# Nine sampling rounds for 128 pixels instead of rounds of 14 pixels, in a deformable-convolution network

## The chip, the cores and the metric

The kernel runs on one core of a Trainium2 chip. The metric is the device time of one execution in microseconds; the kernel before takes 7738.43 us, the median of three runs (7737.99 to 7746.72). Times inside the kernel come from one profiled execution.

## The reference

Four layers work on four images of 256 channels and 64x64 pixels, in float32. The change lies in the first layer, a deformable convolution. Each pixel has four groups of 64 channels, and in each group nine sampling points. Every point has an offset and a softmax weight, both computed from the image; it is a bilinear sample, a weighted sum of the four pixels around a place that is not on the grid.

```python
offset = jnp.einsum('nhwc,oc->nhwo', t, off_w) + off_b
mask = jax.nn.softmax(mlog.reshape(n, H, W, G, P), -1).reshape(n, H, W, G * P)
...
img = xpad.transpose(0, 3, 1, 2).reshape(n * G, GC, Hp, Wp)
samp = _grid_sample(img, sg)
...
dout = (samp * mr).sum(-1).reshape(n, G * GC, H * W).transpose(0, 2, 1).reshape(n, H, W, C)
dout = jnp.einsum('nhwc,oc->nhwo', dout, outproj_w) + outproj_b
x2 = _bn(inp + dout, bn2_g, bn2_b, bn2_m, bn2_v, 3)
```

After it come a squeeze-and-excite with a two-layer feed-forward, a linear-attention layer with 5x5 depthwise convolutions, a binarised 3x3 convolution and a non-local attention layer, each with a group norm before it.

## The kernel before

An earlier stage computes, for each image, a table `tab` in DRAM with 256 values for every place and group (the four pixels of a bilinear sample), and a list `s_d` with one row per pixel and point: four row numbers of the table, one for each group, and 16 weights (four groups, four corners). Rows of `s_d` are ordered by pixel, nine in a row for each.

`sample` then goes through an image in rounds. A round takes RP = 14 pixels, that is RS = 126 rows of `s_d`, one on each of 126 partitions. `gathered` (L596) issues four indirect DMAs on POOL (L600), one for each group, each of which fetches 128 rows of 256 values into a buffer `g`; there are seven such buffers. Partitions 126 and 127 fetch rows of the next round, and their weights in the mask are zero. PE then multiplies `g` by weights `wm` (L607): `wm` has one column for each of OB = 16 pixel slots, and in it the weight of a row stands in the column of its pixel (the mask `own`), so that the matmul sums the nine points and one pair of corners. One round is eight such matmuls, into one half of the accumulator `acc`; two rounds (UR = 2) share a half.

`weigh` (L585) makes `wm` for WR = 4 rounds at once on DVE (L591, 128x1024), in one of two buffers, four rounds ahead. After each pair of rounds three steps follow, one slot apart: `moved` (ACT copies the half of `acc` to SBUF, L612), `turned` (PE transposes it into a half of `dp`, L617) and `spread` (ACT copies it into `dT`, two copies of 64 partitions, L632). When a block of BR = 16 rounds (BP = 224 pixels; the last block of an image has 64 pixels in five rounds) is complete, `project` multiplies `dT` by the output projection (PE, L640), `add` adds the residual (DVE, L644) and `finish` applies the batch norm (ACT, L649) and stores the block as `x2` (SP, L652). `dT` has one buffer, so the first `spread` of the next block waits until `project` has read it, and is put one slot later (`j == 2 and r < UR`). An image has 18 blocks of 16 rounds and one of five, 293 rounds; four images have 1172.

`load` (L572) brings the rows of a block from `s_d` into `sl` with two SP transfers (L580 for partitions 0 to 125, L581 for 126 and 127); it is called one block ahead, and `sl` has two buffers. Because L581 reads two rows past the end, `s_d` has 2 x 126 rows more, filled with zeros in `setup` (L249).

The order of instructions on PE, DVE, ACT and POOL is the order in which the program writes them (`manual_schedule` in `run`). A slot is one round: first the steps that fall due in it (`later`), then the gathers and matmuls of the round, then `load` and `weigh`, and then a share of other layers' work. That share comes from `beside` (L1194): work of the other layers is cut into pieces with a cost each and spread evenly over the rounds. Beside image 0 run the first convolution of images 1 to 3 and the offsets of all images; beside image 1 the binarisation of a weight and, from image 0, the feed-forward (first fifth) and the linear attention (the rest); beside images 2 and 3 also the third and fourth layers of images 0 and 1. The total of that work does not depend on the number of rounds. After the last round the rest of images 2 and 3 runs without sampling.

Of the kernel before, what the change touches and what calls it, by code (L numbers as in the profile page):

```python
# [9 lines left out]
F32 = mybir.dt.float32  # L10
# [15 lines left out]
CT = 8  # L26
# [3 lines left out]
RP, WR, UR, BR = 14, 4, 2, 16  # L30
RS, BP = RP * PT, RP * BR
BLOCKS = [(p0, min(BP, HW - p0)) for p0 in range(0, HW, BP)]
OB = 16
# [38 lines left out]
class Net:  # L72
# [127 lines left out]
    def setup(self):  # L200
# [46 lines left out]
        self.s_d = [dt([HW * PT + 2 * RS, G * 5], F32, name=f"sd{n}") for n in im]  # L247
        for n in im:
            nc.sync.dma_start(self.s_d[n][HW * PT:].rearrange("(p r) f -> p (r f)", r=2), self.zero[0:RS, 0:G * 10])  # L249
# [251 lines left out]
    def coordinates(self, bp, n, c, off, ml):  # L501
# [43 lines left out]
        for xt, wx in ((0, w0[:, 0]), (1, loc[:, 0])):  # L545
# [5 lines left out]
            self.s_d[n][0:HW * PT].rearrange("(t p q) f -> p t (q f)", p=P, q=PT)[:, c * CT:(c + 1) * CT, :],  # L551
# [4 lines left out]
    def sample(self, n, ssum):  # L556
# [15 lines left out]
        def load(b):  # L572
            p0, np_ = BLOCKS[b]
            whole, part = np_ // RP, np_ % RP

            nr = whole + (part > 0)
            sl = sp.tile([P, BR, G * 5], F32, name="sl")
            rows = self.s_d[n][p0 * PT:p0 * PT + nr * RS, :].rearrange("(r p) f -> p r f", p=RS)
            more = self.s_d[n][p0 * PT + RS:p0 * PT + (nr + 1) * RS, :].rearrange("(r p) f -> p r f", p=RS)
            nc.sync.dma_start(sl[0:RS, 0:nr], rows)  # L580
            nc.sync.dma_start(sl[RS:P, 0:nr], more[0:P - RS])  # L581
            rounds = [(r, RP) for r in range(whole)] + [(whole, part)] * (part > 0)
            blocks[b] = sl, rounds

        def weigh(b, r):  # L585

            sl, rounds = blocks[b]
            nu = min(WR, len(rounds) - r)
            wm = self.gp.tile([P, WR, 4 * G, OB], F32, name="wm")
            sh = [P, nu, 4 * G, OB]  # L590
            nc.vector.tensor_tensor(  # L591
                wm[:, 0:nu], self.con("own").unsqueeze(1).unsqueeze(1).to_broadcast(sh),
                sl[:, r:r + nu, G:].unsqueeze(3).to_broadcast(sh), ALU.mult)
            return wm
# [15 lines left out]
        def moved(acc, nu, u):  # L610
            at[u] = sp.tile([P, UR, P], F32, name="at")
            nc.scalar.copy(at[u].rearrange("p v c -> p (v c)")[:, 0:nu * P], acc[:, 0:nu * P])  # L612

        def turned(nu, u):
            dp[u] = next(dps).rearrange("p (v g s o) -> p v g s o", v=UR, g=G, s=2)
            for v in range(nu):
                nc.tensor.transpose(dp[u][:, v].rearrange("p g s o -> p (g s o)"), at[u][:, v], self.ident)  # L617

        def spread(unit, b, u):

            if b not in dT:
                p0, np_ = BLOCKS[b]
                dT[b] = sp.tile([P, G, BP], F32, name="dT", bufs=1)
                images[b] = sp.tile([P, KT, BP], F32, name="yb")
                nc.sync.dma_start(images[b][:, :, 0:np_], self.y_d[n][:, :, p0:p0 + np_])
            full = sum(1 for _, m in unit if m == RP)
            for v0, v1, m in ((0, full, RP), (full, len(unit), unit[-1][1])):
                for s in range(2):
                    if v0 < v1:
                        hs = slice(64 * s, 64 * s + 64)  # L630
                        q0 = RP * (unit[0][0] + v0)
                        nc.scalar.copy(  # L632
                            dT[b][hs, :, q0:q0 + m * (v1 - v0)].rearrange("p g (v o) -> p g v o", o=m),
                            dp[u][hs, v0:v1, :, s, 0:m].rearrange("p v g o -> p g v o"))

        def project(b, m):
            np_ = BLOCKS[b][1]
            po[m] = self.ps("po")
            for k in range(G):
                nc.tensor.matmul(po[m][:, 0:np_], self.ow[:, k, m * P:(m + 1) * P], dT[b][:, k, 0:np_], start=k == 0, stop=k == G - 1)  # L640

        def add(b, m):
            ym = images[b][:, m, 0:BLOCKS[b][1]]
# [699 lines left out]
```

## Time and profile before

| What | us |
| --- | --- |
| median of the timed runs | 7738.43 |
| span of the profiled execution, first to last instruction | 8805.8 |
| before the first gather | 134.1 |
| gathers, first start to last start | 134.1 to 7306.6 |
| rest, without gathers | 7308 to 8805.8 |
| POOL busy | 5152.4 (59%) |
| PE busy | 5993.9 (68%) |
| DVE busy | 5173.3 (59%) |
| ACT busy | 2183.8 (25%) |

The profiled execution is longer than the timed runs, so a time read from it belongs to it and is carried over to the runs only with an argument. In lines of the profile, a group has its line, engine, operation, what it writes and reads with partitions x elements, its count, then its busy time and the mean of one in ns, then the engine's idle time just before it and what ended most of that. A wait line has the engine and line, what released it, the sum in us, the number of times and the longest. A float32 matmul shows as two records.

### The profile page before, as it was taken

To read this page: it belongs to the slowest core of one execution; us is meant where nothing else is said; L and a number is where in the kernel's file an instruction comes from. 1 tells how busy PE (TensorE), PEld (TensorE's weight loads), DVE (VectorE), ACT (ScalarE), POOL (GpSimd) and SP (SyncE) were. 2 spreads that over 40 slices of the span, in tenths; PEclk is the share of its full clock that TensorE was granted. 3 is DMA by queue.
4 is the path that set the end of the run, shared out by engine and by line. 5 is a ranking of instruction groups with operands and counts; after the bars stand their busy time and mean duration, and the time that the engine had idled before them with its cause. 6 is when DMAs were issued, how large, how long until landed. Compare 5 with 4: busy or idle time off the path is not lost. (4 is left out here: it accounts for less than half of the span.)

```text
span 8805.8 us, 95736 instructions
## 1 busy us (share of the span) xinstructions
PE 5993.9 (68%) x36532; PEld 3575.6 (41%) x36532; DVE 5173.3 (59%) x6409; ACT 2183.8 (25%) x4899; POOL 5152.4 (59%) x4950
## 2 busy tenths in 40 slices
PE   4454554448744446688876677888766778986899
PEld 2222222224323322244544443345544433664477
DVE  5444443443466667424777776227777772599834
ACT  1111111112211112122223222222222222465524
POOL 2666666566666666666666656666666661376410
PEclk7676766669866667799988888898878888998999
DMA  6454454444433334444443344444434343220131
GB/s 172 127 155 124 141 154 118 125 145 145 153 105 105 110 105 129 127 130 138 134 135 110 112 121 136 142 134 132 136 115 117 114 118 99 69 74 29 48 98 53
DMA packets 759050, 1042.27 MB, mean 118 GB/s; under 512 B 362432, under 2 KB 472128, under 8 KB 757056
## 3 DMA queue, kind: packets, MB, share of 16 engines
q0 software_dynamic: 225024, 614.77, 24.3%
q1 hardware_dynamic: 533568, 421.39, 16.4%
q8 instruction: 289, 4.73, 0.2%
q14 instruction: 169, 1.38, 0.0%
HBM read 867.08 MB, written 168.69 MB: 118 GB/s over the span
## 5 line engine op out<-in xcount | busy, mean ns | idle before, releaser
L600 POOL DMA_INDIRECT g<-tab,sl x4688 | 4618.5, 985 | 2687.8 <-issue 1224.2
L178 DVE SCALAR_TENSOR_TENSOR agg<-pad,vec,agg 128x1024 f32<-128x1024 f32 x2280 | 2933.5, 1287 | 61.9
L607 PE MATMUL acc<-g,wm 128*32 128x128 f32 x18752 | 1034.8, 333 | 1907.8 <-ACT at L612 1273.7
L607 PEld LDWEIGHTS acc<-g,wm 128*32 128x32 f32 x18752 | 566.8, 128 | 2411.7 <-ACT at L612 1446.1
L1048 PE MATMUL ps<-xd,w 128*128 128x256 f32 x3072 | 752.7, 396 | 51.3 <-issue 37.8
L591 DVE TENSOR_TENSOR wm<-con,sl 128x1024 f32<-128x1024 f32 (+1 forms) x296 | 357.7, 1209 | 711.9 <-remote 533.5
L1048 PEld LDWEIGHTS ps<-xd,w 128*128 128x128 f32 x3072 | 595.1, 199 | 175.0 <-issue 86.0
L632 ACT COPY dT<-dp 64x112 f32<-64x112 f32 x1176 | 285.9, 243 | 1043.7 <-remote 544.3
L742 PE MATMUL ps<-x2f,f 128*128 128x512 f32 x1024 | 499.2, 636 | 19.1 <-issue 7.7
L817 PE MATMUL ps<-xr,qw 128*128 128x512 f32 x768 | 472.0, 746 | 22.1 <-issue 11.1
L727 DVE SCALAR_TENSOR_TENSOR hm<-ps,vec,lk 128x512 f32<-128x512 f32 x256 | 190.8, 750 | 492.9 <-ACT lk L744 405.5
L752 PE MATMUL ps<-hm,f 128*128 128x512 f32 x1024 | 467.1, 605 | 0.9 <-DVE hm L727 0.9
L612 ACT COPY at<-acc 128x256 f32<-128x256 f32 (+1 forms) x588 | 218.3, 371 | 986.3 <-remote 753.2
L999 POOL TENSOR_TENSOR xd<-xp 128x640 f32<-128x640 f32 x64 | 79.4, 1268 | 492.6 <-ACT xp L1011 298.3
L640 PE MATMUL po<-dT,ow 128*128 128x224 f32 (+1 forms) x1216 | 326.1, 419 | 45.4 <-issue 19.3
L617 PE MATMUL dp<-ident,at 128*128 128x128 f32 x1172 | 284.1, 330 | 106.6 <-ACT dT L632 61.0
L865 ACT COPY kt<-pt 128x512 f32<-128x512 f32 x256 | 149.4, 584 | 829.3 <-remote 403.8
L744 ACT ACTIVATE lk<-ps,low 128x512 f32<-128x512 f32 x256 | 174.0, 687 | 666.0 <-PE ps L742 512.1
L1147 PE MATMUL s<-ph,th 128*128 128x512 f32 x512 | 290.2, 672 | 62.5 <-ACT kt L865 15.9
L640 PEld LDWEIGHTS po<-dT,ow 128*128 128x128 f32 x1216 | 265.5, 233 | 113.8 <-issue 68.9
L1167 PEld LDWEIGHTS ps<-gt,pT 128*128 128x128 f32 x2048 | 276.0, 213 | 70.8 <-issue 46.1
L194 POOL TENSOR_TENSOR ak<-ak,m 128x1024 f32<-128x1024 f32 x96 | 228.1, 2376 | 130.6 <-ACT m L193 126.7
(243 smaller groups left out, 8022.0 us busy)
## 6 DMA issues: line engine op xcount, KB each, us to landing
g<-tab,sl POOLq DMA_INDIRECT x4688
x<-x SPq DMA_DIRECT2D x128, 512.0 KB
xr<-x SPq DMA_DIRECT2D x96, 512.0 KB
tab<-xo SPq DMA_DIRECT2D x192, 128.0 KB
x<-in_x SPq DMA_DIRECT2D x32, 512.0 KB
y<-yc SPq DMA_DIRECT2D x32, 512.0 KB
x2f<-x SPq DMA_DIRECT2D x32, 512.0 KB
xyf<-x SPq DMA_DIRECT2D x32, 512.0 KB
```

What stands on the lines that cost most here:

```text
L178: nc.vector.scalar_tensor_tensor(to, s, wt, acc, ALU.mult, ALU.add)
L591: nc.vector.tensor_tensor(wm[:, 0:nu], self.con("own").unsqueeze(1).unsqueeze(1).to_broadcast(sh), sl[:, r:r + nu, G:].unsqueeze(3).to_bro ...
L600: nc.gpsimd.indirect_dma_start(out=g[:, i, :], out_offset=None, in_=table, in_offset=bass.IndirectOffsetOnAxis(ap=sl.bitcast(I32)[:, r, i: ...
L607: nc.tensor.matmul(acc[32 * i:32 * i + 32, :], wm[:, r4, 4 * i + 2 * x:4 * i + 2 * x + 2, :], g[:, i, x * P:(x + 1) * P], start=x == 0, st ...
L617: nc.tensor.transpose(dp[u][:, v].rearrange("p g s o -> p (g s o)"), at[u][:, v], self.ident)
L632: nc.scalar.copy(dT[b][hs, :, q0:q0 + m * (v1 - v0)].rearrange("p g (v o) -> p g v o", o=m), dp[u][hs, v0:v1, :, s, 0:m].rearrange("p v g ...
L640: nc.tensor.matmul(po[m][:, 0:np_], self.ow[:, k, m * P:(m + 1) * P], dT[b][:, k, 0:np_], start=k == 0, stop=k == G - 1)
L742: nc.tensor.matmul(ps, f1[:, k, m * P:(m + 1) * P], x2[:, k], start=k == 0, stop=k == KT - 1)
L752: nc.tensor.matmul(ps, f2[:, k, m * P:(m + 1) * P], hm[:, k], start=k == 0, stop=k == 4 * KT - 1)
L817: nc.tensor.matmul(ps, qw[:, k, m * P:(m + 1) * P], x[:, k], start=k == 0, stop=k == KT - 1)
L1048: nc.tensor.matmul(ps[:, e], w[:, k, t, 2 * half + e, m * P:(m + 1) * P], v[:, 2 * half + e, k, t:t + 8], start=i % 6 == 0, stop=i % 6 == 5)
L1147: nc.tensor.matmul(s[i], tv[:, 4 * b + j], ph[:, i * 512:(i + 1) * 512], start=True, stop=True)
```

## The change

An image is cut into 32 groups of 128 pixels (GP), and a group into nine rounds. In each round the first 126 rows carry 14 pixels as before. The 126 pixels of nine rounds leave two of the group's pixels; each of these has nine points, and round r takes point r of both on partitions 126 and 127. The mask `own` gives these two rows columns of their own, 14 and 15, so every one of the 128 rows that a gather fetches is used. The two pixels' results are then spread over nine rounds, as nine partial sums in columns 14 and 15 of `dT`; a new step `shared` adds them up (DVE reduces over the rounds, ACT writes the sum into the first round's place).

A block is two groups: 18 rounds, 256 pixels, 16 blocks in an image, no partial block; 288 rounds in an image, 1152 in all, 4608 gathers. `weigh` makes three rounds at once (128x768) instead of four. `load` has four transfers for a block instead of two, and `s_d` needs no zero rows. `spread` copies 16 columns a round instead of 14, `project` works on 288 columns instead of 224, `add` is two instructions instead of one. `shared` falls due three slots after a block's last round, `project`, `add` and `finish` two slots later than before, and the first `spread` of the next block three slots after its usual place instead of one.

```diff
-RP, WR, UR, BR = 14, 4, 2, 16
-RS, BP = RP * PT, RP * BR
-BLOCKS = [(p0, min(BP, HW - p0)) for p0 in range(0, HW, BP)]
-OB = 16
+RP, WR, UR, BG = 14, 3, 2, 2
+RS, GP = RP * PT, RP * PT + 2
+BR, BP, OB = PT * BG, GP * BG, RP + 2
+NBLK = HW // BP
...
-        self.s_d = [dt([HW * PT + 2 * RS, G * 5], F32, name=f"sd{n}") for n in im]
-        for n in im:
-            nc.sync.dma_start(self.s_d[n][HW * PT:].rearrange("(p r) f -> p (r f)", r=2), self.zero[0:RS, 0:G * 10])
+        self.s_d = [dt([HW * PT, G * 5], F32, name=f"sd{n}") for n in im]
...
         def load(b):
...
-            nc.sync.dma_start(sl[0:RS, 0:nr], rows)
-            nc.sync.dma_start(sl[RS:P, 0:nr], more[0:P - RS])
...
+            blocks[b] = sl = sp.tile([P, BR, G * 5], F32, name="sl")
+            for h in range(BG):
+                rows = self.s_d[n][(b * BG + h) * GP * PT:(b * BG + h + 1) * GP * PT]
+                to = sl[:, h * PT:(h + 1) * PT]
+                nc.sync.dma_start(to[0:RS], rows[0:RS * PT].rearrange("(r p) f -> p r f", p=RS))
+                nc.sync.dma_start(to[RS:P], rows[RS * PT:].rearrange("(p r) f -> p r f", r=PT))
...
             wm = self.gp.tile([P, WR, 4 * G, OB], F32, name="wm")
-            sh = [P, nu, 4 * G, OB]
+            sh = [P, WR, 4 * G, OB]
...
+            for s in range(2):
+                hs = slice(64 * s, 64 * s + 64)
+                nc.scalar.copy(dT[b][hs, :, r:r + UR], dp[u][hs, :, :, s, :].rearrange("p v g o -> p g v o"))
+
+        def shared(b):
+            v = dT[b].rearrange("p g (h r) o -> p (g h) o r", r=PT)
+            both = sp.tile([P, G * BG, 2], F32, name="both")
+            nc.vector.tensor_reduce(both, v[:, :, RP:], AX.X, ALU.add)
+            nc.scalar.copy(v[:, :, RP:, 0], both)
...
         def add(b, m):
-            ym = images[b][:, m, 0:BLOCKS[b][1]]
-            nc.vector.tensor_tensor(ym, po[m][:, 0:BLOCKS[b][1]], ym, ALU.add)
+            ym = images[b][:, m].rearrange("p (h q) -> p h q", h=BG)
+            pm = po[m][:, 0:BR * OB].rearrange("p (h r o) -> p h r o", h=BG, o=OB)
+            y4 = ym[:, :, 0:RS].rearrange("p h (r o) -> p h r o", o=RP)
+            nc.vector.tensor_tensor(y4, pm[:, :, :, 0:RP], y4, ALU.add)
+            nc.vector.tensor_tensor(ym[:, :, RS:], pm[:, :, 0, RP:], ym[:, :, RS:], ALU.add)
...
-                todo = [(i + 1 + j + (j == 2 and r < UR), f) for j, f in enumerate(todo)]
-                if ends:
-                    todo += [(i + 4 + m + j, partial(f, b, m)) for m in range(KT) for j, f in enumerate((project, add, finish))]
+                todo = [(i + 1 + j + (j == 2 and r < UR) * (6 - 3), f) for j, f in enumerate(todo)]
+                if r == BR - 1:
+                    todo += [(i + 3, partial(shared, b))]
+                    todo += [(i + 6 + m + j, partial(f, b, m)) for m in range(KT) for j, f in enumerate((project, add, finish))]
...
-        "own": p[:, None] // PT == np.arange(OB)[None],
+        "own": np.where(p < RS, p // PT, p - RS + RP)[:, None] == np.arange(OB)[None],
```

## The prediction

> **What bounds the kernel now.** I read the head of the page and its costliest groups first, then the busy times by stretch, then the waits of POOL, then the timeline. From the page:
>
> ```profile
> span 8805.8 us, 95736 instructions
> ...
> L600 POOL DMA_INDIRECT g<-tab,sl x4688 | 4618.5, 985 | 2687.8 <-issue 1224.2
> ...
> L607 PE MATMUL acc<-g,wm 128*32 128x128 f32 x18752 | 1034.8, 333 | 1907.8 <-ACT at L612 1273.7
> ...
> L591 DVE TENSOR_TENSOR wm<-con,sl 128x1024 f32<-128x1024 f32 (+1 forms) x296 | 357.7, 1209 | 711.9 <-remote 533.5
> L632 ACT COPY dT<-dp 64x112 f32<-64x112 f32 x1176 | 285.9, 243 | 1043.7 <-remote 544.3
> ...
> L640 PE MATMUL po<-dT,ow 128*128 128x224 f32 (+1 forms) x1216 | 326.1, 419 | 45.4 <-issue 19.3
> ```
>
> The gathers are 4688 instructions of 985 ns, 4 in each of 1172 rounds. Busy times by stretch (columns: stretch, length, then PE, PEld, DVE, ACT, POOL busy, granted clock, DMA share, GB/s); the cuts are the four images' gathers, the last three images split where the feed-forward work beside them ends:
>
> ```profile
> 134.00:1912.00 1778.00, 839.24 (x6643) 480.56 (x6643) 787.45 (x1041) 248.35 (x689) 1165.60 (x1172) 0.66 0.48 137
> 1912.00:2270.00 358.00, 278.95 (x1475) 136.10 (x1476) 126.49 (x183) 73.11 (x176) 231.09 (x226) 0.88 0.50 149
> 2270.00:3667.00 1397.00, 758.48 (x5341) 412.19 (x5341) 926.71 (x873) 266.81 (x693) 930.22 (x948) 0.70 0.40 116
> ...
> 4030.00:5487.00 1457.00, 1066.04 (x7090) 676.63 (x7091) 1058.59 (x1248) 378.73 (x933) 915.80 (x937) 0.85 0.44 126
> 5487.00:5850.00 363.00, 301.43 (x1559) 142.25 (x1558) 87.36 (x123) 75.47 (x175) 227.98 (x234) 0.91 0.46 135
> ...
> 7308.00:8805.00 1497.00, 1310.58 (x5370) 871.99 (x5368) 950.99 (x1409) 658.51 (x1072) 533.18 (x256) 0.94 0.21 67
> ```
>
> The reader is to see that PE's and DVE's work differs by a factor of two between stretches, while a round takes about the same everywhere: 1778 us over 293 rounds is 6.07 us, 1397 over 237 is 5.9, 1457 over 234.25 is 6.2, 363 over 58.5 is 6.2. What is the same in all of them is the four gathers. POOL's own waits:
>
> ```profile
> POOL g L600 <- issue: 1224.2, 4007, 0.7
> POOL g L600 <- remote: 624.7, 307, 6.0
> POOL g L600 <- PE acc L607: 494.3, 201, 23.2
> ```
>
> "Issue" is 1224.2 / 4007 = 0.30 us before each gather. So a gather occupies POOL for 0.985 + 0.30 = 1.285 us, a round for 5.14 us, all 4688 for 6024 us. The gathers run from 134 to 7308 us, 7174 us in all, so 1150 us are waits: POOL has filled its seven buffers g and waits for PE.
>
> **Profile and runs.** The profiled execution took 8805.8 us from first to last instruction, the timed runs 7738.43 in the median: 1067 us less. Head, unbroken gathers and tail make 134 + 6024 + 1497 = 7655 us, 83 short of the median. My reading, an estimate from these numbers: the timed runs have few of the 1150 us of waits, and POOL is their bound nearly throughout. The other reading, that all is stretched by 8805.8 / 7738.43 = 1.138, is used as a check below.
>
> **Removed.** 4096 pixels in groups of 128 make 32 groups of nine rounds, 288 rounds instead of 293 for each image: 20 rounds and 80 gathers less over four images. On POOL this is 80 x 1.285 = 103 us. By the whole profiled round it is 20 x 7174 / 1172 = 122 us of the profiled span, or 122 / 1.138 = 108 us of a run: the two readings agree. Off POOL, PE loses 20 x 16 matmul records of 1034.8 / 18752 = 55 ns, 18 us, off the path. The four zero fills at setup go, but the first block's load has two transfers more: taken as nothing, within 2 us by SP's issue of 1.1 us.
>
> **Weights (L591).** 296 instructions over 1024 columns become 384 over 768. The nearest row is the two-input 128x768 of L290, 958 ns: 384 x 0.958 = 368 us, 10 us more on DVE. It also holds POOL up. In the timeline:
>
> ```profile
> 3013.16 0.94 POOL L600 DMA_INDIRECT g<-tab,sl  x1 [0.30 <-issue]
> 3014.27 1.22 DVE L591 TENSOR_TENSOR wm<-con,sl 128x1024 f32<-128x1024 f32 x1 [8.53 <-remote]
> 3014.40 1.91 POOL L600 DMA_INDIRECT g<-tab,sl  x1 [0.30 <-issue]
> ```
>
> The gather that meets the weights takes 1.91 us instead of 0.95. Over all gathers this excess is 4688 x (985 - 946, the median) = 183 us. If it goes with DVE's busy time it grows by 3%, 5 us; if with the number of weight instructions, by 88 / 296, 54 us. The held gather outlasts the weights by under a microsecond, so length counts more than number: I take 10 us. The Trainium skill ("SBUF — State Buffer", section "Who interferes with whom") speaks here in two ways: a two-input DVE instruction keeps GpSimd's reads out for its whole length, yet it infers that such an instruction does not stall descriptor writing. By the first half the sum would carry about 10 us, an estimate; by the inference nothing; the row above contradicts the inference.
>
> **Residual add (L644).** 152 instructions of 388 ns (57 us) become 128 pairs: 252 columns at 414 ns (L1032, 128x256), and four columns for which the nearest rows are 164 ns (L1157) and 298 ns (L1156), both 128x1. That is 74 to 91 us; with 250 ns it is 85, DVE +28.
>
> **The new sum of the nine parts.** 64 reductions of 144 columns to 16; the row of twice that size (L539) is 447 ns, so 164 to 447 ns and I take 300: DVE +19. 64 ACT copies of 16 columns at about 0.2 us (L649's one-column read 189 ns, 64 columns at L470 244 ns): 14 us. ACT's L632 becomes 1152 copies of 128 columns, about 12 ns longer each by L470's 244 and 293 ns: ACT +9. ACT is busy 25% of the span, so both are hidden in its idle time. L640: 1024 matmul records of 288 columns for 1216 of 224, each between 268 ns (unchanged) and 268 x 288 / 224 = 345: 274 to 353 us against 326, hidden except as below.
>
> **Loads.** Four SP transfers a block instead of two, 256 for 152: at L581's 1.1 us at most 115 us of SP's time. What stands behind them in SP's queue is the side work's block loads and the x2 stores, double buffered, at most 2.2 us later once a block. The block's rows are needed 18 rounds, 92 us, after they are asked for. Nothing; without that lead, 2.2 x 64 = 141 us.
>
> **Order.** Projection, add and finish go two slots later, the first spread of the next block too, and in the slot of the last spread ACT must wait for DVE's reduction. Behind that copy on ACT stands the move of the next block's first two rounds, PE's transposes wait for that, and PE's gathered matmuls stand behind them. Later, in the eighth round, PE's transpose needs the half of dp that ACT frees in the same slot, behind finish and DVE's add. I cost this at nothing: when PE is late, POOL goes on into seven buffers, 7 x 5.14 = 36 us. If POOL already stands at the seventh, the price passes through (third rival).
>
> **Where the sum is not full.** In the feed-forward stretches PE is busy 301 us over 58.5 rounds, 5.15 us a round, as much as POOL's 5.14. One round fewer there in each of three images brings nothing: +15 us. In the two late stretches DVE would be busy 1059 / (234.25 x 5.14) = 88% at POOL's pace; of the 57 us that DVE gains half falls there, and a quarter to a third of it may show: +8, between 0 and 57.
>
> **Sum.** -103 + 10 + 15 + 8 = -70 us: 7668. Its own ends are -103 (7635) and -103 + 54 + 15 + 57 = +23 (7761).
>
> **Rivals.** (1) PE and DVE bind in images 1 to 3, and the side work that they carry does not shrink. For it: the 88% and 89% (1066 of 1204 us) above. Against: rounds cost the same where DVE has half the work. Only image 0 gains, 5 x 5.14 = 26 us, and half of three quarters of DVE's 57 us shows, 21: 7733, no change.
>
> (2) Slower, by the new chain spread, reduction, copy, move, transpose at each block's end. For it: PE's gathered matmuls already wait for L612, 1273.7 us, and POOL stands at its seventh buffer in the profiled execution. Its price, by the 35 waits of PE for L632 (115.8 us, 3.3 us each): 64 x 3.3 = 212 us, less 103: 7847. It decides from 103 / 64 = 1.6 us that reaches POOL per block. Against it: 36 us of buffers, and the 83 us that the median leaves for all waits.
>
> (3) The rounds are not fewer, or a load runs late so that the saved gathers become waits for sl: 7738. Against: the only wait for sl is the start's 132.8 us.
>
> **Chances.** Forecast 0.68, (1) 0.12, (2) 0.17, (3) 0.03. A measurement of this kernel tells about 0.2%, 15.5 us, from no change. A little of the forecast's upper end is no change, so faster 0.68, same 0.14, slower 0.18. The range of 8 in 10 goes from 7632, just under the forecast's full gain, to 7760, its upper end, which takes in (1) and (3) and leaves most of (2) out.
>
> **What would show it.** 4608 gathers, POOL's sum near 4540 us and its mean still near 985 ns; 384 weight instructions near 0.96 us; the last gather some 100 to 125 us earlier in the profile, the tail still about 1497 us. Wrong if the mean gather rises by over 12 ns (the hold), if POOL's waits for PE grow by more than 100 us, or if they gather once in 18 rounds, just after a block's end (rival 2). If the stretches of images 2 and 3 keep their length, rival 1 is right.

## The result and the profile after

The kernel after takes 7745.95 us in the median (12 runs, 7735.88 to 7753.6), the kernel before 7737.6 us in the runs beside it (12 runs, 7732.43 to 7746.72). The ratio is 1.0005, with a 95% interval of 0.9998 to 1.0013: no change, where 7668 us and a gain were forecast.

One thing has to be known to read the profiles. The profile of before that the prediction used must have come from another chip than the timed runs: on two other chips the kernel before takes 8816 and 8817 us without any profiling, at the clock of that profile and with its waits. So the two kernels were profiled again beside each other on one chip of the 7738 us kind (runs before_third and after_again), and all that follows rests on these two executions, unless it says otherwise. The one of after is the longest of its ten runs (7760.0 us, median 7750.62). Groups of the kernel before:

```profile
span 7744.6 us, 95736 instructions
...
L600 POOL DMA_INDIRECT g<-tab,sl x4688 | 4603.0, 982 | 1656.5 <-issue 1313.6
...
L591 DVE TENSOR_TENSOR wm<-con,sl 128x1024 f32<-128x1024 f32 (+1 forms) x296 | 357.2, 1208 | 395.9 <-PE acc L607 365.1
```

The same groups of the kernel after, and PE's projection:

```profile
span 7758.2 us, 94959 instructions
...
L591 POOL DMA_INDIRECT g<-tab,sl x4608 | 4499.1, 976 | 1766.8 <-issue 1259.5
...
L598 PE MATMUL acc<-g,wm 128*32 128x128 f32 x18432 | 1264.5, 321 | 1233.9 <-ACT at L603 720.9
...
L582 DVE TENSOR_TENSOR wm<-con,sl 128x768 f32<-128x768 f32 x384 | 365.3, 952 | 421.8 <-PE acc L598 404.5
...
L618 ACT COPY dT<-dp 64x128 f32<-64x128 f32 x1152 | 296.7, 258 | 1036.3 <-PE dp L608 707.2
...
L631 PE MATMUL po<-dT,ow 128*128 128x288 f32 x1024 | 315.9, 458 | 14.9 <-ACT dT L626 7.9
```

POOL (GpSimd) works 104 us less on the gathers (4603.0 to 4499.1): 79 us for the 80 gathers that are gone, and the rest because the mean gather is 6 ns shorter. Its idle time before them is 110 us longer (1656.5 to 1766.8). The waits of POOL, before and then after, say for what:

```profile
POOL g L600 <- issue: 1313.6, 4310, 0.6
...
POOL g L600 <- PE acc L607: 126.0, 110, 8.2
```

```profile
POOL g L591 <- issue: 1259.5, 4132, 0.6
...
POOL g L591 <- PE acc L598: 282.5, 181, 9.0
```

The short pauses shrink by 54 us. Of these 24 go with the 80 gathers; the others stand before gathers that now wait for something by name. The waits for PE more than double, by 157 us. Where these lie shows when the span is cut at the first gather of each image. Columns as in the prediction: stretch, length, PE, PEld, DVE, ACT and POOL busy, clock, DMA share, GB/s; the rows are images 0 to 3 and the tail. The kernel before:

```profile
134.70:1659.38 1524.68, 998.31 (x6726) 530.59 (x6726) 798.32 (x1060) 250.22 (x692) 1159.65 (x1173) 0.70 0.56 160
1659.38:3177.60 1518.22, 1121.91 (x6851) 560.79 (x6852) 1045.97 (x1046) 345.70 (x877) 1154.14 (x1172) 0.79 0.49 142
3177.60:4719.51 1541.91, 1262.00 (x8656) 771.79 (x8658) 1141.31 (x1372) 455.19 (x1108) 1145.60 (x1172) 0.91 0.52 151
4719.51:6260.78 1541.27, 1264.35 (x8662) 771.62 (x8655) 1141.06 (x1372) 455.09 (x1108) 1143.59 (x1172) 0.91 0.51 149
6260.78:7744.60 1483.82, 1296.30 (x5280) 866.54 (x5278) 946.45 (x1402) 653.52 (x1061) 533.41 (x256) 0.94 0.21 66
```

The kernel after:

```profile
132.73:1626.76 1494.03, 967.35 (x6598) 504.51 (x6598) 801.87 (x1115) 253.38 (x693) 1134.31 (x1152) 0.70 0.57 162
1626.76:3123.27 1496.51, 1104.65 (x6717) 547.71 (x6718) 1055.79 (x1117) 348.15 (x872) 1128.47 (x1152) 0.79 0.48 142
3123.27:4693.06 1569.79, 1258.10 (x8537) 759.94 (x8536) 1149.34 (x1436) 458.49 (x1103) 1120.24 (x1152) 0.90 0.50 147
4693.06:6267.24 1574.18, 1258.23 (x8517) 759.39 (x8516) 1148.91 (x1435) 457.58 (x1100) 1116.08 (x1152) 0.90 0.49 144
6267.24:7758.20 1490.96, 1302.13 (x5266) 864.20 (x5264) 949.41 (x1403) 653.95 (x1059) 533.28 (x257) 0.93 0.21 66
```

Images 0 and 1 became 31 and 22 us shorter, about what five rounds of 5.14 us are worth. Images 2 and 3 became 28 and 33 us longer, though each has five rounds fewer, and though no engine has noticeably more to do there (VectorE +8 us, TensorE -4 to -6, GpSimd -25 to -28). The tail took 7 us more. With 2 us less at the start the parts sum to +14 us, the difference of the two spans. In the other profiled execution of the kernel after (7735.88 us) images 0 and 1 are the same, images 2 and 3 took 1566 and 1562 us, so 24 and 21 us longer than before, and the tail took no longer than before. The direction does not hang on the execution, but single images differ by up to 12 us between two executions of one kernel. So the saving was made and lost again, and the question is what images 2 and 3 have that 0 and 1 have not.

### The profile page after: what moved, and what is told of

It is laid out like the page before. It is cut to its first block, busy times and chain, and to the rows that moved or that the text cites. A ratio compares the mean times of both kernels' runs of the same rounds, so it can differ in the third digit from the quotient of the medians.

```text
span 7734.1 us, 94959 instructions
## 1 busy us (share of the span) xinstructions
PE 5939.0 (77%) x36000; PEld 3468.1 (45%) x36000; DVE 5191.6 (67%) x6665; ACT 2200.4 (28%) x4879; POOL 5026.2 (65%) x4870
## 5 line engine op out<-in xcount | busy, mean ns | idle before, releaser
L591 POOL DMA_INDIRECT g<-tab,sl x4608 | 4492.3, 975 | 1757.4 <-issue 1273.2
L598 PE MATMUL acc<-g,wm 128*32 128x128 f32 x18432 | 1266.6, 319 | 1241.6 <-ACT at L603 711.0
L598 PEld LDWEIGHTS acc<-g,wm 128*32 128x32 f32 x18432 | 623.2, 121 | 1927.9 <-ACT at L603 951.2
L582 DVE TENSOR_TENSOR wm<-con,sl 128x768 f32<-128x768 f32 x384 | 365.8, 953 | 420.3 <-PE acc L598 400.7
L618 ACT COPY dT<-dp 64x128 f32<-64x128 f32 x1152 | 296.7, 258 | 1044.3 <-PE dp L608 705.6
L603 ACT COPY at<-acc 128x256 f32<-128x256 f32 x576 | 214.4, 372 | 490.0 <-PE acc L598 477.9
L631 PE MATMUL po<-dT,ow 128*128 128x288 f32 x1024 | 312.2, 455 | 13.4 <-ACT dT L626 6.5
L1155 PE MATMUL ps<-gt,pT 128*128 128x128 f32 x2048 | 291.0, 302 | 7.1 <-ACT pT L1151 7.0
L730 PEld LDWEIGHTS ps<-x2f,f 128*128 128x128 f32 x1024 | 191.3, 194 | 230.1 <-issue 216.9
L194 POOL TENSOR_TENSOR av<-av,m 128x1024 f32<-128x1024 f32 x96 | 226.9, 2363 | 101.1 <-ACT m L193 96.7
```

Source lines behind the costliest of these rows:

```text
L194: nc.gpsimd.tensor_tensor(acc, acc, m, ALU.add)
L582: nc.vector.tensor_tensor(wm, self.con("own").unsqueeze(1).unsqueeze(1).to_broadcast(sh), blocks[b][:, r:r + WR, G:].unsqueeze(3).to_broad ...
L591: nc.gpsimd.indirect_dma_start(out=g[:, i, :], out_offset=None, in_=table, in_offset=bass.IndirectOffsetOnAxis(ap=sl.bitcast(I32)[:, r, i: ...
L598: nc.tensor.matmul(acc[32 * i:32 * i + 32, :], wm[:, r4, 4 * i + 2 * x:4 * i + 2 * x + 2, :], g[:, i, x * P:(x + 1) * P], start=x == 0, st ...
L618: nc.scalar.copy(dT[b][hs, :, r:r + UR], dp[u][hs, :, :, s, :].rearrange("p v g o -> p g v o"))
L631: nc.tensor.matmul(po[m][:, 0:BR * OB], self.ow[:, k, m * P:(m + 1) * P], dT[b][:, k].rearrange("p r o -> p (r o)"), start=k == 0, stop=k ...
```

## The experiments

Ratios are against the kernel before, on the same chip and in the same session. Lengths of images are from first gather to next first gather (for image 3, to the end of the last gather), read from the one profiled execution of each run; the medians are of 4 to 12 runs.

| Run | median us | before | ratio, 95% | images 0, 1, 2, 3 in us | tail |
| --- | --- | --- | --- | --- | --- |
| before_third | 7746.42 (one run) | 7743.24 | | 1525, 1518, 1542, 1541 | 1484 |
| after (first profile) | 7745.95 | 7737.6 | 1.0005 (0.9998 to 1.0013) | 1494, 1496, 1566, 1562 | 1483 |
| after_again | 7750.62 | 7743.24 | 1.0007 (0.9997 to 1.0016) | 1494, 1497, 1570, 1574 | 1491 |
| b_288_second | 7747.56 | 7743.24 | 1.0004 (0.9995 to 1.0014) | 1495, 1498, 1570, 1561 | 1486 |
| a_noshared_second | 7732.35 | 7743.24 | 0.9985 (0.9975 to 0.9995) | 1494, 1500, 1569, 1557 | 1489 |
| a_pace293 | 7758.64 | 7742.49 | 1.0022 (1.0012 to 1.0032) | 1491, 1496, 1553, 1580 | 1502 |
| a_pace300 | 7774.15 | 7742.49 | 1.0043 (1.0027 to 1.006) | 1486, 1498, 1537, 1583 | 1535 |
| b_pace288 | 7812.83 | 7742.49 | 1.01 (1.0083 to 1.0117) | 1521, 1513, 1587, 1585 | 1465 |
| a_second1 | 7799.13 | 7742.49 | 1.0073 (1.0056 to 1.009) | 1494, 1493, 1564, 1604 | 1511 |
| a_second79 | 7792.37 | 7735.72 | 1.0066 (1.0048 to 1.0084) | 1490, 1500, 1590, 1597 | 1481 |
| b_second79 | 7781.8 | 7735.72 | 1.0051 (1.0031 to 1.007) | 1522, 1516, 1558, 1560 | 1491 |
| a_second70 | 7852.0 | 7735.72 | 1.015 (1.0132 to 1.0168) | 1491, 1493, 1619, 1619 | 1476 |
| a_light | 7653.29 | 7737.64 | 0.9886 (0.987 to 0.9903) | 1492, 1493, 1534, 1534 | 1464 |
| b_light | 7702.23 | 7737.64 | 0.9947 (0.9931 to 0.9964) | 1522, 1518, 1534, 1532 | 1464 |
| hybrid | 7705.58 | 7737.64 | 0.9951 (0.9935 to 0.9968) | 1490, 1520, 1528, 1541 | 1492 |

### Which chip the first profile came from

before_again is the unchanged kernel before.

> The kernel before once more, for a second profile: the first one's span, 8805.8 us, is 1067 us over the timed runs, while the profile after has a span of 7734.1. Theory A (the first profile was disturbed; undisturbed, POOL runs almost without a break): a span near 7740, a round of 5.2 us over 1172 rounds, POOL's waits for PE under 100 us beyond 0.3 us a gather. Rival (the kernel before always waits as the first profile shows, and the profiled execution is just slower): a span near 8800, rounds of 6.1 us.

Measured: 8793.3 us, with eleven runs of the kernel before beside it at 8817.05 us in the median. So the 1067 us between the first profile and the timed runs were not the cost of profiling: this chip takes them without it. Two experiments ran there first, b_288 and a_noshared; both were repeated on a chip of the other kind with the two unchanged kernels beside them, and only the repetition can be laid beside the result.

### Fewer rounds alone: b_288

The kernel before with only its 18 full blocks. The last 64 pixels of an image are copied instead of sampled, so the rounds are 288 and each round, each weight and each order is that of before.

```diff
-BLOCKS = [(p0, min(BP, HW - p0)) for p0 in range(0, HW, BP)]
+BLOCKS = [(p0, BP) for p0 in range(0, HW - BP + 1, BP)]
+REST = HW % BP
...
+        yr = sp.tile([P, KT, REST], F32, name="yr", bufs=1)
+        nc.sync.dma_start(yr, self.y_d[n][:, :, HW - REST:])
+        nc.sync.dma_start(self.x2_d[n][:, :, HW - REST:], yr)
```

> The kernel before with only its 18 full blocks in each image: the last 64 pixels of an image are left out of the sampling (their residual is copied instead), so that there are 288 rounds as in the changed kernel, and the side work is spread over 288. Theory A (a round is worth POOL's 5.14 us, and the change gives it back elsewhere): 7738 - 103 = 7635 us, ratio 0.987. Rival B (side work on DVE and PE binds, and it packs tighter when there are fewer rounds): 7715 to 7745, ratio 0.997 to 1.001.

There: 8774.04 us, ratio 0.9941 (0.9924 to 0.9957).

> The kernel before with 288 rounds an image, its last 64 pixels left out of the sampling. On the 8817 us chip it took 0.994 of the kernel before. On a 7738 us chip, theory A (a round is worth POOL's 5.14 us): 7635, 0.987. Rival B (the side work of some stretches binds, and with fewer rounds more of it falls on each): 7690 to 7745, 0.994 to 1.001.

On the chip of the 7738 us kind: 7747.56 us, ratio 1.0004 (0.9995 to 1.0014). It saves the rounds and has none of the new steps, and its images are those of the kernel after within 3 us, but for image 3, which is 13 us shorter (and as long as in the first profile of after, 1562 us). So the new sampling is not what took the saving away. Taking five rounds from an image that also carries the linear and the fourth layer makes that image longer by itself. And all that the new sampling does otherwise (its weights, its sum, its later places) comes to 3 us net, the difference of the two medians.

### The new step alone: a_noshared

The kernel after without `shared` (reduction and copy); the two extra pixels of each 128 keep only the first of their nine points.

```diff
-                    todo += [(i + 3, partial(shared, b))]
```

> The changed kernel without the step that adds the nine partial sums (DVE reduction and ACT copy, 64 of each): for two pixels of each 128 only the first point's part is used. Theory S (the chain spread, reduction, copy, move, transpose at each block's end holds PE and through it POOL): most of the 103 us comes back, 7650 to 7690 us. Rival (that chain is hidden; the time goes to the side work): 7730 to 7750.

There: 8764.49 us, ratio 0.9935 (0.9918 to 0.9952).

> The changed kernel without the adding up of the nine partial sums (two pixels of 128 keep only their first point's part). On a 7738 us chip, theory S (the reduction's chain at each block's end costs): 7650 to 7690. Rival B: 7730 to 7748, the same as the changed kernel within 15 us.

Here: 7732.35 us beside the 7750.62 us of the kernel after, so the step costs 18 us of time, 0.3 us a block. It is a cost, and not the missing saving, which is some 100 us. Where in the image it lies cannot be read: image 3 is 17 us shorter here and image 2 only 1, but image 3 differs by 12 us between the two profiles of the kernel after.

A further run, a_lag1, was to put the projection and the next block's first spread back into their old places. It has no time: in that order the engines would wait for one another without end. So what the later places cost was not measured apart.

### The two kernels side by side: after_again and before_third

> The changed kernel again, on whatever chip this is. One chip ran the kernel before in 7738 us and another in 8817. On a chip of the first kind all theories expect a ratio of 1.000 (7738 to 7750 us). On one of the second kind, where the profile of before showed POOL waiting for PE in most rounds: theory P (there the round as a whole has a price, and fewer rounds save it) 0.990 to 0.995; rival (the change costs at the blocks' ends as much as it saves on any chip) 0.998 to 1.002.

> The kernel before, for its profile beside the changed kernel's on the same chip. If the chip is of the 7738 us kind, theory A: a span near 7736, gathers from 134 to about 6250 us, a round of 5.2 us over 1172 rounds, and POOL's waits for PE near 110 us beyond 0.3 us a gather, about 100 us less than the 218 of the changed kernel. Rival (the tail without gathers got longer in the changed kernel): waits like the changed kernel's, but a tail some 100 us shorter than its 1483.

Their profiles are those shown above. Theory A's number for the span came true (7744.6 us, the last gather ending at 6260.8, 126.0 us of waits for PE), and a tail that grew by 100 us is ruled out (1484 us before, 1491 after).

### The pace of the side work: a_pace293, a_pace300, b_pace288, a_second1

`beside` spreads the other layers' pieces over a given number of rounds. With fewer rounds, more of them fall into each. In a_pace293 and a_pace300 the kernel after spreads the work of images 2 and 3 as if there were 293 or 300 rounds, and what is left over comes at once behind the image's last round; in b_pace288 the kernel before, with its sampling untouched, spreads it as if there were 288; in a_second1 the fourth layer may use the rounds to the end.

```diff
-                    beside(self.sample(n, ssum[n]), rounds, *behind(n - 1), (second(n - 2), SECOND, 0.2, 0.9))
+                    beside(self.sample(n, ssum[n]), 293, *behind(n - 1), (second(n - 2), SECOND, 0.2, 0.9))
```

> The changed kernel with the side work of images 2 and 3 spread as over 293 rounds while there are 288: each round carries as much as in the kernel before, and the last 1.7% of it runs after the image's last round. In the changed kernel images 2 and 3 take 1576 and 1574 us, in the kernel before 1542 and 1541, images 0 and 1 are 31 and 22 us shorter. Theory D (each round's side work, 1.7% more of it, is what binds in images 2 and 3): they shrink to 1490 to 1530 us each, 7640 to 7700 in all. Rival E (what the change itself adds on DVE, ACT and PE binds): no gain, 7735 to 7760.

> As a_pace293, but spread as over 300 rounds, 4% less side work in a round than in the changed kernel and that 4% (some 45 us of DVE work an image) after the image's rounds. Theory D (density): the rounds get a little faster still, but the rest without gathers costs 20 to 40 us an image: 7660 to 7740. Theory Q (no density, but two pieces of other layers that happen to fall on the same rounds at about four fifths of an image): the time goes up or down without order, anywhere from 7640 to 7800, and the slow rounds move to another place.

> The kernel before, its sampling untouched at 293 rounds, with the side work of images 2 and 3 spread as over 288: 1.7% more in each round, done five rounds before the image's end. Theory D: images 2 and 3 get 20 to 50 us longer each, 7780 to 7840 in all, with the slow rounds at four fifths of the image as in the kernels of 288 rounds. Rival E (the number of rounds and what the sampling adds set the time, not the pace of the side work): 7730 to 7750.

> The changed kernel with the third and fourth layers' work beside images 2 and 3 ended at the end of the image instead of at 0.9 of it. The rounds between 0.79 and 0.94 of image 2 took 5.5 to 6.8 us with DVE busy 4.9 to 5.9 us of each, the last twelve 5.05 with DVE at 2.3. Theory D: the load on the crowded rounds falls by an eighth of that work, images 2 and 3 shrink to 1500 to 1540 each, 7660 to 7710 in all. Rival E: 7735 to 7760.

b_pace288 is the clearest: the sampling and the side work are the same, only 1.7% more side work stands in each round of images 2 and 3, and these grow by 45 and 43 us, the whole by 70. The slack of before is that thin. In the other direction the looser pace does shorten image 2 (1570, 1553, 1537), but what is left over is then done at the end: image 3 becomes 6 and 9 us longer and the tail 11 and 44, and the sum is a loss. a_second1 too: image 2 gains 6 us, image 3 and the tail lose 50. So of theory D's four numbers only that of b_pace288 came true; for the three edits of the kernel after it was too low by 59, 34 and 89 us, and a_pace293 came out at rival E's number. Theory Q, pieces that happen to meet, has a_pace300's 7774 us in its range, and the slow rounds of image 2 begin there at 0.86 of its rounds instead of 0.80, so Q is not excluded. In a_pace293 each round carries as much side work as before, and yet image 2 took 5.39 us a round (1553 / 288), where before has 5.26. So the pace is enough to push before over the edge, but to loosen it is not enough to bring after back.

Where in the image is it lost? Two stretches of image 2 by equal shares of its rounds, 0.2 to 0.8 (the linear layer's depthwise beside the fourth layer) and 0.8 to 0.92 (the linear layer's output, L904, beside the fourth layer). The kernel before, 172 and 37 rounds:

```profile
3497.80:4388.70 890.90, 712.34 (x5423) 503.03 (x5422) 785.97 (x952) 280.35 (x693) 675.77 (x688) 0.89 0.52 151
4388.70:4601.70 213.00, 176.46 (x1102) 95.36 (x1101) 183.34 (x217) 70.82 (x170) 143.69 (x149) 0.91 0.45 132
```

The kernel after, 169 and 36 rounds:

```profile
3436.60:4339.50 902.90, 695.12 (x5271) 486.91 (x5269) 776.90 (x979) 279.55 (x687) 657.74 (x677) 0.88 0.51 147
4339.50:4572.20 232.70, 187.25 (x1141) 100.94 (x1142) 198.01 (x237) 72.47 (x172) 138.44 (x144) 0.89 0.40 117
```

At the 5.18 us a round that before shows in the first stretch (890.9 / 172), after would take 875 us there; it takes 28 more. In the second it takes 20 us more than before instead of one round less. DVE is busy 88% and 86% in the two rows of before, 86% and 85% in those of after. That is not as full as it can be: in the second stretch of a_second79, below, it is 96%. That it stays lower here because its instructions wait, in their written order, for PE and ACT was not tried.

POOL's waits for PE in the two stretches, before and then after:

```profile
POOL g L600 <- PE acc L607: 14.6, 20, 3.4
POOL g L600 <- PE acc L607: 28.5, 14, 4.3
```

```profile
POOL g L591 <- PE acc L598: 50.4, 39, 6.7
POOL g L591 <- PE acc L598: 57.4, 22, 6.3
```

The seven buffers explain a part of this. Counted in the traces, POOL is in image 2 (from 0.3 to 0.8 of its rounds) on average 3.1 rounds ahead of PE's matmuls in before and 5.6 in after, where six is the most that the buffers allow. In images 0 and 1 it is 1.0 in both. So before comes to the second stretch with some three rounds of buffers free, and after with almost none. Just ahead of it (0.75 to 0.8) it is 2.9 in before, which takes 213 us there, and 1.8 in b_light, which takes 205. It is 5.6 in after, 5.6 in b_288_second and b_pace288 and 5.7 in a_light, which take 227 to 244. No run changed the number of buffers, so this is a reading and not a test.

So the missing time has two places, and two explanations were open: a crowd of two works at one place (A), or no room in the images at all (B).

### A crowd, or no room: a_second79, b_second79, a_second70

The fourth layer is ended where the linear layer's output begins (0.79), in both kernels, or earlier still (0.7).

```diff
-                    beside(self.sample(n, ssum[n]), rounds, *behind(n - 1), (second(n - 2), SECOND, 0.2, 0.9))
+                    beside(self.sample(n, ssum[n]), rounds, *behind(n - 1), (second(n - 2), SECOND, 0.2, 0.79))
```

> The kernel after, with the fourth layer's work of images 2 and 3 spread over the shares 0.2 to 0.79 of an image's rounds instead of 0.2 to 0.9, so that it has ended where the linear layer's output begins (rounds 230 to 265 of 288). Theory A, a crowd: the 28 and 33 us that images 2 and 3 lose are lost only because two works meet in those rounds; without the meeting images 2 and 3 fall to some 1515 us each (288 rounds by 5.26 us), and the time to 7640 to 7690 us. Theory B, no room: VectorE's and TensorE's work for images 2 and 3 is as long as POOL's rounds over the whole image, so that work taken out of rounds 230 to 265 makes rounds 60 to 227 slower by as much; images 2 and 3 stay at 1560 to 1590 us and the time at 7730 to 7800 us.

> The kernel before, with the same edit. Theory A, a crowd: the kernel before lost a little there too (its images 2 and 3 are 17 and 24 us longer than images 0 and 1), so 10 to 40 us faster than before. Theory B, no room: no faster than before, and rounds 60 to 230 longer than the 5.1 us that they took. By either theory the kernel after with this edit, less this one, is the number to read: about minus 80 us by A, about 0 by B.

> The kernel after, with the fourth layer's work of images 2 and 3 spread over the shares 0.2 to 0.7, tighter still: 40% more of it in each round than with 0.2 to 0.9. Theory A, a crowd: as with 0.79, or a few us slower. Theory B, no room: rounds 60 to 200 become longer by tens of us, rounds 200 to 287 shorter, and images 2 and 3 together are no shorter than 3140 us.

The same two stretches of image 2 in a_second79:

```profile
3438.50:4401.60 963.10, 756.82 (x5531) 536.82 (x5530) 796.80 (x1037) 305.45 (x745) 658.83 (x676) 0.89 0.49 140
4401.60:4596.80 195.20, 150.79 (x944) 67.54 (x944) 187.19 (x191) 52.67 (x127) 140.63 (x145) 0.87 0.52 157
```

The crowd is gone: its 36 rounds fall from 232.7 to 195.2 us. The first stretch pays 60 us for these 37.5. With 0.7 the first stretch takes 1002 us. A falls, and B's numbers stand but for image 3, 7 us above its upper end: work taken from one place of images 2 and 3 comes back, with interest, at another. The kernel before with the edit is 46 us slower, where A had 10 to 40 us faster, and after less before with the same edit is 10.6 us, not minus 80. B's reason, that VectorE's and TensorE's work itself fills the rounds, is less sure: in that first stretch DVE is busy 83% and PE 79%.

### Is it VectorE's work? a_light and b_light

> The kernel after, with 4 of the 25 instructions of each 5x5 depthwise of the linear layer working on the upper half of their rows only (L178; the lower half keeps the sum without these four points); the costs by which the work is spread stay. That takes about 96 times 0.64 us = 61 us of VectorE's time out of images 2 and 3 each, and changes nothing of POOL's rounds nor of where work is put. Theory B, no room beside shorter rounds: images 2 and 3 fall from 1570 and 1574 us to 1500 to 1530 us, so by 40 to 70 us each. Theory A, a crowd of TensorE and ScalarE alone: by less than 20 us each. The tail, which has the same layer, is read apart.

> The kernel before, with the same edit. Theory B: its rounds are longer, so VectorE has nearly room there already, and images 2 and 3 fall from 1542 us by 15 to 30 us only, to POOL's pace (some 1515 to 1525 us): with the lighter VectorE the kernel after is ahead in every image, by 15 to 30 us each, 60 to 110 us in all. Theory A: less than 20 us each here as well, and the kernel after stays behind in images 2 and 3.

```diff
-                nc.vector.scalar_tensor_tensor(to, s, wt, acc, ALU.mult, ALU.add)
+                hf = rows // 2 if out is not None and t % 5 == 4 and t < k * k - 1 else rows
+                nc.vector.scalar_tensor_tensor(to[:, 0:hf], s[:, 0:hf], wt, acc[:, 0:hf], ALU.mult, ALU.add)
```

With the same edit the kernel after takes 7653.29 us and the kernel before 7702.23: now the change is worth 49 us. Images 2 and 3 fall by 36 and 40 us in the kernel after (by 32 and 27 from its first profile) and by 8 and 9 in the kernel before. They then take the same in both kernels (1534 and 1534 us, 1534 and 1532), so the 49 us are the saving of images 0 and 1: the loss is gone, but five rounds fewer still bring nothing in images 2 and 3. Theory B had expected 15 to 30 us there for each. The first stretch of image 2, a_light and then b_light:

```profile
3433.80:4308.10 874.30, 686.67 (x5271) 482.17 (x5269) 738.56 (x979) 279.38 (x687) 657.73 (x677) 0.90 0.53 152
```

```profile
3494.90:4387.00 892.10, 728.22 (x5450) 513.15 (x5449) 753.98 (x960) 281.70 (x698) 674.66 (x688) 0.89 0.53 151
```

In the kernel after 38 us less of DVE (776.9 to 738.6) bring 29 us of time, down to 5.17 us a round, POOL's pace, and POOL's waits for PE fall from 50.4 to 16.8 us. In the kernel before 32 us less (786.0 to 754.0) bring nothing (890.9 and 892.1): there POOL set the pace. So in this stretch before stood just on one side of the edge and after on the other. Theory B's number for a_light was not quite reached (1534 us, with 1500 to 1530 expected): the crowd between 0.8 and 0.92 still takes 227.1 us, only 5.6 less, though DVE has 8 us less to do there, so that stretch is not VectorE's amount of work alone; PE is busy 183.9 us of it. It is there that the rounds saved in images 2 and 3 are lost: a_light is 18 us shorter than b_light in the first stretch and 22 us longer here (227.1 against 204.6). What binds in it was not settled.

### The saving where it is real: hybrid and hybrid_one

Images 0 and 1 sampled as in the kernel after, images 2 and 3 as in the kernel before.

```diff
+        with self.tc.tile_pool(name="gather16", bufs=2, side="left") as self.gp, \
+                self.tc.tile_pool(name="samp16", bufs=2, side="left") as self.sp:
+            with ordered():
+                for n in range(2, N):
+                    beside(self.sample16(n, ssum[n]), sum(-(-n_ // RP) for _, n_ in BLOCKS16), *behind(n - 1), (second(n - 2), SECOND, 0.2, 0.9))
```

> Images 0 and 1 sampled as in the kernel after (288 rounds, all 128 rows), images 2 and 3 as in the kernel before (293 rounds); everything else as it was. If the saving is real where POOL sets the pace, and the loss comes only from shorter rounds in the images that carry the linear and the fourth layer together, images 0 and 1 take 1494 and 1497 us and images 2 and 3 1542 us each: 53 us less than before, 7675 to 7700 us, ratio 0.992 to 0.995. If something else in the kernel after lost the time (the tail, the state left by images 0 and 1), it stays near 7740 us.

Measured: 7705.58 us, ratio 0.9951 (0.9935 to 0.9968): faster than the kernel before by 32 us, and some 6 us above the upper end expected. Of the 53 us, POOL lost 25 at the seam; image 2 behind it was 14 us shorter than in before, so not all of the 25 were lost time, and the tail was 8 us longer. Its timeline there, before and behind the seam:

```profile
3115.89 0.94 POOL L596 DMA_INDIRECT g<-tab,sl  x1 [0.30 <-issue]
3142.14 1.43 POOL L726 DMA_INDIRECT g<-tab,sl  x1 [25.31 <-DMA sl<-sd]
```

The first load of image 2 into the new buffers came 25 us late. hybrid_one shares one set of buffers instead, with the weights of images 2 and 3 made three rounds at a time.

> As the hybrid before it (images 0 and 1 with 288 rounds and all 128 rows, images 2 and 3 with 293 rounds of 14 pixels), but the two kinds of sampling share one set of buffers, so that image 2 does not start behind the release of image 1's buffers, where GpSimd stood still for 25 us; to fit, the weights of images 2 and 3 are made three rounds at a time instead of four (110 instructions per image instead of 74). If that standstill was lost time, some 20 us less than the hybrid's 7705 us: 7680 to 7695 us, ratio 0.992 to 0.9945. If images 2 and 3 merely took it up (their VectorE work had a head start while GpSimd stood), the time stays at 7700 to 7715 us.

It ran on a slower chip: 8799.1 us beside 8815.78 us, ratio 0.9974 (0.996 to 0.9987). There POOL stood for 2.2 us at the seam, so the standstill is gone, but what it is worth cannot be read from another chip's time, and stays open.

## Why the prediction was wrong

**Profile and runs.** The reading was right that the timed runs have few of the first profile's waits (126 us for PE, not 494), and POOL's 6024 us for all gathers is near what was found: 4688 gathers took 6126.1 us from the first to the last (134.7 to 6260.8). The longer profile was most likely another chip's.

**Removed.** Right for images 0 and 1, which got about what five rounds each are worth. That POOL's busy time fell by 104 us where the term is 103 is chance: the term is 79 of busy time and 24 of pauses, and the other 25 us of busy time come from the shorter mean gather. The last gather, forecast 100 to 125 us earlier, ended 6 us later.

**Weights.** Right in size: 365.3 us for 368 expected, so DVE +8. The hold that was feared did not grow: the gather's mean fell from 982 to 976 ns while the weight instructions rose from 296 to 384, and b_288_second, with the weights of before and as many gathers as after, has 978. So the 10 us charged for it were not seen. By the inference of the Trainium skill ("SBUF — State Buffer", "Who interferes with whom"), that a two-input DVE instruction does not stall descriptor writing, the sum would carry nothing, and that was nearer. The forecast's row, a gather of 1.91 us, does not clearly contradict the inference: a gather's row numbers stand in `sl` in SBUF, and the same section says that such an instruction contends with GpSimd's reads of SBUF.

**Residual add and the new sum.** 52.6 + 19.3 us for the pair (L637 411 ns, L638 151 ns), 72 for 85 expected; the reduction (L625) is 387 ns for 300, its copy (L626) 205 ns for 200. By their rows DVE has 48 us more in place of 57; its busy time in all rose by 32. (The old add is 374 ns in the mean, not 388; the 57 us of the forecast are right.)

**Loads.** Right: after the start no gather of the kernel after waits for `sl`.

**Order and rival 2.** The chain exists, as big as that rival made it, and was mostly hidden, as the forecast had it:

```profile
ACT dT L618 <- PE po L631: 321.6, 60, 16.1
...
ACT dT L626 <- DVE both L625: 216.3, 64, 15.9
```

216.3 us over 64 blocks are 3.4 us each, 3.3 expected. Without the whole step the time is only 18 us less (a_noshared_second), where the forecast had nothing. The first wait was 43.3 us in the kernel before; that the later place of the projection makes it was not shown. Together with all else that is new it comes to 3 us net (b_288_second), and what it costs apart stays open. The buffers that were to hide such delays were mostly free in images 0 and 1 only; in images 2 and 3 POOL stood at 5.5 of the six rounds that it can be ahead.

**Where the sum is not full.** This step failed. It saw that DVE would be busy 88% of the late stretches at POOL's pace, and took 12% of it for room, so that a quarter to a third of DVE's added work would show: +8 us, at most 57. Measured, images 2 and 3 came out 28 and 33 us longer (24 and 21 in the other profile of after), where the forecast's terms have each about 14 shorter (five rounds, 26, less 5 for the feed-forward round, 4 of the 8 here, 2.5 of the weights' 10). That is 89 us more (73 by the other profile), so the term that was set at 8 us measured some 80 to 97. The bound was wrong too, because it counted only the work that the change adds to DVE. What costs is the old side work, which has to go through in 26 us less an image. b_288_second shows it with no work added, b_pace288 with nothing but the spreading changed. a_light and b_light show that VectorE's load decides on which side of the edge a kernel stands in the first of the two stretches where the time is lost; for the second the cause stays open. The forecast's own sign of being wrong came: POOL's waits for PE grew by 157 us, over the 100 that it allowed.

The other half of the step, 15 us for three feed-forward rounds that bring nothing, was half right. The first 60 rounds of images 1, 2 and 3 took 326, 313 and 316 us in after, the first 61 in before 321, 320 and 321: 7 us less in all, where three rounds at POOL's pace are 15, and image 1 became longer.

**Rival 1** had the right place, PE and DVE in the late images, and nearly the right time (7733 against 7746), the latter by luck, since it had not the right signs: image 1 did gain, and images 2 and 3 did not keep their length, they lost. "Rounds cost the same where DVE has half the work" was the argument held against it. It is true of before (5.2 us against 5.26), and says only that before had not yet crossed the edge, not how far off the edge was.

## What to carry to other kernels

A bound that holds by a few per cent over the next one is worth only those few per cent, and work woven in beside it by rounds gets denser when the rounds get fewer. A busy share of 86 to 88% does not say how much room an engine has whose instructions, in their written order, wait for others (here there was none at that share, though in another stretch the same engine reached 96%). How many buffers stand full says more: in the kernel before POOL ran 1.0 round ahead of PE in the images where the saving was real and 3.1 in those where it was not. Before taking work off the engine that sets the pace, spread the side work a little denser in the unchanged kernel and see whether it still fits (b_pace288). Where only some stages have room, make the change only in these (hybrid).

## What the runs showed of the hardware that was not expected

Chips differ. The kernel before took 7736 to 7743 us in the sessions of one kind, on three chips or more, 8816 and 8817 us on two other chips, 14% more; each of these two was seen in one session, so whether it is the chip or a lasting state of it is not shown. The granted clock was 0.849 against 0.808, which is 5%. The engines' own work hardly differs: in image 1 on the slower chip (1758 us against 1518) POOL was busy 1156.6 us against 1154.1 and DVE 1052.8 against 1046.0, and PE even less, 1045 against 1122. What differs is waiting, 459 to 494 us of POOL for PE and 625 to 628 that the profile cannot name ("remote"), against 126 us. On the slower chip fewer rounds alone did help (b_288, 0.6%), on the others not: one and the same change has two answers. Why was not tried.
